# Third layer of a four-layer cross-attention stack: two kinds of stores are issued by ScalarE, and a load is issued later in SyncE's queue

## The chip, the core and the metric

The kernel runs on one core of a Trainium2 chip, in one launch. The metric is the device time of that launch in microseconds (us), as the median of several runs. The engines are TensorE (PE; its weight loads are listed as PEld), VectorE (DVE), ScalarE (ACT), GpSimd (POOL) and SyncE (SP), which in this kernel issues every DMA before the change. Each engine takes its instructions in the order in which they were built and waits at an instruction until the semaphores that it names are reached.

## What is computed

An input x of 8 x 256 tokens with 512 features goes through four cross-attention layers against a context of the same size. In the reference, the third one (the one that changes) reads, with the mask added to the scores:

```python
q = hidden_state @ Wq + bq            # 32 heads of 16
k = encoder_hidden_state @ Wk + bk    # 8 key heads of 16, each for 4 query heads
v = encoder_hidden_state @ Wv + bv
scores = jnp.einsum('bkgld,bksd->bkgls', q, k) * scale + mask
attn = jax.nn.softmax(scores, axis=-1)
out = jnp.einsum('bkgls,bksd->bkgld', attn, v)
out = out @ Wo + bo
x = out + hidden_state                # then a layer norm with gamma and beta
```

The first layer has 16 heads with a feed-forward part, the second a single head, the fourth 16 heads with a layer norm on the context and a gated sum.

## The kernel before, in words

The program is written with a tile framework: pools hand out buffers by tag, and the framework inserts the semaphores. A DMA reports its landing on one of eight completion semaphores, which are handed out in turn to the DMAs of all queues; a DMA is issued only when the last user of its semaphore has landed. A scheduler that runs a timeline at build time decides the order on each engine where the program does not pin it.

The attention of layers one, three and four runs in `pipeline(units, ...)`. A unit of the third layer (`Gqa`) is one of the 8 batch rows `b` and one of four groups `ft` of eight query heads and two key heads, so there are 32 units. The pipeline moves in steps `t` of four chunks. In step `t` it does part A of unit `t`, part B of unit `t-1` and part C of unit `t-2`, and lays other work (projections, the second layer, the contexts, the fourth layer's inputs) between the chunks as fillers under a budget. In steps 2 to 25 TensorE's order is pinned to the written one (`keep_order`); from step 26 the scheduler chooses.

- `load` (L1252, L1253): two loads bring queries into a `stack` tile and keys into a `ks` tile; two stack tiles take turns.
- `A(h)` (L1262, L1272, L1285): products of queries and keys into two "sm" banks, a masked maximum by VectorE, and the negated maxima as a high and a low part in `mhl`.
- `B` (L1293 to L1296): TensorE transposes `mhl`, ScalarE copies it to `mT`, and a DMA writes it as four extra rows, 96 to 99, into the stack tile, so that the next product already has the maxima subtracted.
- `C(i)` (L1315 to L1330): products into two "st" banks, the mask added either by VectorE (L1328) or, after a copy by ScalarE (L1325), by GpSimd (L1326), then ScalarE's exponential (L1330) into a tile `P` or `pk`.
- `D` (L1351 to L1362): the value product `AV` (L636) into the one "av" bank; ScalarE copies it to `xt` (L1355), a DMA stores it to DRAM as `avd` (L1356), and two DMAs load it back as `nd` (L1360), sums and divisors side by side in another layout. These loads wait until the store has landed.
- `E`, some 18 us of planned time later: ScalarE takes the reciprocal of the divisors by two table functions (L1368, L1369), GpSimd multiplies and splits (L1370 to L1373).

Other DMAs of the stage that SyncE issues in the same queue: the stores of keys `k2d` (L1129, six for a batch row) and of queries `q2d` (L422, six) out of two staging tiles `nat`, the loads of the transposed context (L1096) into the same staging tiles, weights (L200), masks (L1578, L1579), and the layer's output (L1528). Before it fills a staging tile (L417 for queries), ScalarE waits until the stores out of it have landed.

Of the kernel before, what the change touches and what calls it, by code (L numbers as in the profile page):

```python
# [8 lines left out]
F = mybir.dt.float32  # L9
# [9 lines left out]
P = 128  # L19
# [9 lines left out]
EL2 = 18.0  # L29
# [19 lines left out]
def S(s):  # L49

    o = []
    for p in s.split(","):
# [9 lines left out]
             P="b5,b0-2", V="v1,v0", vo="b7", nat="b8,b9", h="b10", hc="c0-3", xt="c4-7", bc="c8")  # L62
# [13 lines left out]
def tile_xattn_stack(  # L76
# [31 lines left out]
    nc = tc.nc  # L108
# [54 lines left out]
    def dram(shape, name):  # L163
        return tc.dram_tile(shape, F, name=nm(name))

    def fp(ap):
        return ap.bitcast(F)
# [68 lines left out]
    def feat_mm(pt, ws, ft, xs, n=D):  # L236
        run(feat_steps(pt, ws, ft, xs, n))
        return 12 * n * MMUS

    def tok_mm(pt, xs, tt, ws, n=D):  # L240
        run(tok_steps(pt, xs, tt, ws, n))
        return 12 * n * MMUS


    def feat_g(pt, ws, ft, xs, n=D):
        yield from halves(feat_steps(pt, ws, ft, xs, n), 6 * n * MMUS)
# [103 lines left out]
    fill = Fillers()  # L350
# [134 lines left out]
    avd = [[dram([P, D], "avd") for _ in range(4)] for _ in range(NB)]  # L485
# [129 lines left out]
    class Ring:  # L615
# [4 lines left out]
        def next(self):  # L620
            self.i += 1
            return self.ts[self.i % len(self.ts)]

    def flat(t):
        return fp(t).rearrange("p h t -> p (h t)")
# [23 lines left out]
    class Mha:  # L649
# [1 line left out]

        NCH = 4
        US = 0.6
        ELAG = 2.0

        def __init__(self, ph, st, b, ft, qd, kd, vbias):
            self.__dict__.update(ph=ph, st=st, b=b, ft=ft, vbias=vbias)
# [39 lines left out]
        def B(self):  # L697
            ph = self.ph
            mp = ph.PS("pp")
            nc.tensor.transpose(mp[0:16, 0:P], fp(self.mhl.rearrange("p j c -> p (j c)")), ident)  # L700
            mT = ph.T([32, P], R, "mT")[0:16]
            nc.scalar.copy(mT, mp[0:16, 0:P])
            nc.sync.dma_start(out=flat(self.qs)[97:99], in_=fp(mT))
# [62 lines left out]

    def pipeline(units, before, after, budget, ordered=lambda t: False):
        n, lag = len(units), 2
        late, held = [], []
        prev = [None]  # L770

        def keep_order(first):
            for x in nc.cur_bb.bb.instructions[first:]:
                if x.engine == mybir.EngineType.PE:
                    if prev[0] is not None:
                        tc.add_manual_dep(
                            x,
                            prev[0].name,
                            mybir.DependencyInfo(mybir.DependencyClass.NoSync, mybir.DependencyReason.DATA),
                            reason="keep_order",  # L780
                        )
                    prev[0] = x

        def finish(e):
            units[e].D()
            late.append((fill.now + units[e].ELAG, e))

        for t in range(n + lag + 1):
            fill.step = t
            first = len(nc.cur_bb.bb.instructions)  # L790
            if t == 0:
                before(0)
                units[0].load()
            if t + 1 < n:
                before(t + 1)
                units[t + 1].load()
            u = units[t] if t < n else None
            w = units[t - 1] if 0 <= t - 1 < n else None
            v = units[t - lag] if 0 <= t - lag < n else None
            nch = max(z.NCH for z in (u, v) if z) if (u or v) else 4  # L800
            for i in range(nch):
                us = 0.0
                for z, f in ((u, "A"), (v, "C")):
                    if z and i % (nch // z.NCH) == 0:
                        with tc.high_priority(PRIO):
                            getattr(z, f)(i // (nch // z.NCH))
                        us += z.US
                if i == nch // 2 - 1 and w and not ordered(t):
                    w.B()
                fill.tick(us, budget(t) / nch)  # L810
                if i == 0 and w and ordered(t):
                    w.B()
                while held:
                    finish(held.pop())
                while late and late[0][0] <= fill.now:
                    _, e = late.pop(0)
                    units[e].E()
                    after(e)
            if v:
                if ordered(t):  # L820
                    held.append(t - lag)
                else:
                    finish(t - lag)
            if ordered(t):
                keep_order(first)
            else:
                prev[0] = None
        for _, e in late:
            units[e].E()
            after(e)  # L830
# [219 lines left out]
    cb = bcrow(ph2, "cproj_b")  # L1050
    fill.add(a0_fill())
    pipeline(units0, a0_before, a0_after, lambda t: B0 if 2 <= t < len(units0) else B0E)
    fill.drain()
    ff.ph = ph3
# [13 lines left out]
    for x_ in range(2):  # L1068
        nc.sync.dma_start(
            out=w2od.rearrange("(c r x) n -> x c r n", r=16, x=2)[x_],  # L1070
            in_=w2o.rearrange("(c x r) n -> x c r n", x=2, r=16)[x_],
# [167 lines left out]
    class Gqa:  # L1239
# [1 line left out]

        NCH = 4
        US = 0.8
        ELAG = EL2

        def __init__(self, st, kst, b, ft):
            self.__dict__.update(ph=ph5, st=st, kst=kst, b=b, ft=ft)
# [42 lines left out]
        def B(self):  # L1290
            ph = self.ph
            mp = ph.PS("pp")
            nc.tensor.transpose(mp[0:32, 0:P], fp(self.mhl.rearrange("p u j c -> p (u j c)")), ident)  # L1293
            mT = ph.T([32, P], R, "mT")
            nc.scalar.copy(mT, mp[0:32, 0:P])
            nc.sync.dma_start(out=flat(self.qs)[96:100], in_=fp(mT))  # L1296


        def probs(self):
# [48 lines left out]
        def D(self):  # L1348
            self.av = self.ph.PS("av")
            self.AV()  # L1350
            done2[0] += 1  # L1351
            ph = self.ph
            b, ft = self.b, self.ft
            avs = ph.T([P, D], F, "xt")
            nc.scalar.copy(avs, self.av)  # L1355
            nc.sync.dma_start(out=avd[b][ft], in_=avs)  # L1356
            self.nd = ph.T([P, 2, 256], F, "nd")
            dv = avd[b][ft].rearrange("(g n r) (x t) -> n g r x t", g=4, n=2, x=2)
            for n in range(2):
                nc.sync.dma_start(out=self.nd[:, n, :], in_=dv[n])  # L1360
# [205 lines left out]
    units = [Gqa(ring2, ringk, b, ft) for b in range(NB) for ft in range(4)]  # L1566
# [34 lines left out]
    def after(t):  # L1601
        b = (t % n2) // 4
        if t >= n2 and t % 4 == 1:
            res[b] = take_pair(ph6, h2d[b])
        if t % 4 == 3:
            if t < n2:
                fill.add(l2_post(b, units[t].at), hot=True)
            else:
                fill.until(lambda: "o3" in wts)
                fill.add(proj(ph5, b, units[t].at, wts["o3"], res[b], a3_out), hot=True)  # L1610

    pipeline(
        units,
        lambda t: before2(t) if t < n2 else before3(t),
# [105 lines left out]
```

## Time and profile before

| | |
|---|---|
| runs | 1745.91, 1734.97, 1745.66 us, median 1745.66 |
| profiled execution | 1749.12 us; span of the profile 1747.3 us |
| TensorE busy | 1608.8 us (92% of the span) |
| VectorE, ScalarE, GpSimd busy | 1063.5, 877.1, 772.0 us |
| HBM | 230.79 MB read, 96.49 MB written |

All durations below come from the profiled execution, and the runs' median is 3.5 us under it. In the profile's rows, a line such as L1330 is a line of the kernel printed above; "out<-in" are its tiles with the buffer numbers left out; "idle before" is the time that the engine stood ahead of an instruction, with what released it. SPq is SyncE's queue, which is not counted as busy. PEclk is the granted clock of TensorE, 1.00 being full. A wait for a DMA is named after one DMA on the semaphore that came last, which need not be the one that is meant.

### The profile page before, as it was taken

Reading aid. Unit: us, or ns where it says so; the run is one execution under the profiler, and the core shown is the slowest. Engines: PE = TensorE matmul, PEld = TensorE weight load, DVE = VectorE, ACT = ScalarE, POOL = GpSimd, SP = SyncE. Lnnn points to the kernel's source line nnn. Section 1 sums busy time; section 2 is a strip of 40 time slices with the busy share of each in tenths; the row PEclk is TensorE's granted clock in tenths of the full one; section 3 lists DMA queues with packets and bytes.
Section 4 is the critical chain, followed back from the end, with each engine's and each line's share of the span. In section 5 each row is a group of like instructions: output and inputs, shape, how many; then the busy total and the mean of one; then the engine's idle time right before and its main releaser. Section 6 shows DMA issues by size and latency. Waiting matters only on the chain. (4 is left out here: it accounts for less than half of the span.)

```text
span 1747.3 us, 28325 instructions
## 1 busy us (share of the span) xinstructions
PE 1608.8 (92%) x9984; PEld 1231.5 (70%) x9984; DVE 1063.5 (61%) x2380; ACT 877.1 (50%) x1563; POOL 772.0 (44%) x792
## 2 busy tenths in 40 slices
PE   7999998999899999998889989989878999999998
PEld 6877866777667778887666767667556676778765
DVE  5258556777757766632547767767776774644353
ACT  5335545554545565642346655555564555444454
POOL 6345144323465565532225546555564564312111
PEclk9999998999989999999899999999988899999999
DMA  8879675555542534257657467466264656766562
GB/s 295 310 237 295 208 238 186 165 163 163 171 128 77 176 109 150 80 211 239 219 182 235 162 209 237 159 222 199 93 214 137 202 171 208 231 198 212 183 198 66
DMA packets 168444, 329.16 MB, mean 188 GB/s; under 512 B 16336, under 2 KB 84336, under 8 KB 162800
## 3 DMA queue, kind: packets, MB, share of 16 engines
q1 hardware_dynamic: 168304, 327.35, 58.5%
q8 instruction: 80, 1.31, 0.3%
q14 instruction: 60, 0.49, 0.1%
HBM read 230.79 MB, written 96.49 MB: 187 GB/s over the span
## 5 line engine op out<-in xcount | busy, mean ns | idle before, releaser
L688 DVE TENSOR_REDUCE negm<-sm 128x2 f32<-128x512 f32 x256 | 168.9, 682 | 114.2 <-PE sm L681 113.5
L725 ACT ACTIVATE P<-st 128x512 f32<-128x512 f32 x256 | 144.7, 594 | 111.5 <-PE st L717 108.0
L212 PE MATMUL pp<-ys,fw 128*128 128x512 f32 x768 | 192.6, 401 | 7.4 <-ACT fw L178 3.8
L226 PE MATMUL pp<-pw,gs 128*128 128x512 f32 x768 | 192.0, 397 | 2.9 <-ACT gs L1027 2.6
L636 PE MATMUL av<-P,V 128*32 128x256 f32 (+1 forms) x2204 | 173.7, 408 | 6.0 <-ACT P L1330 3.2
L212 PEld LDWEIGHTS pp<-ys,fw 128*128 128x128 f32 x768 | 145.0, 192 | 42.0 <-ACT fw L178 4.0
L212 PE MATMUL pp<-x,wq 128*128 128x256 f32 x1152 | 160.3, 288 | 9.8 <-ACT wq L181 6.3
L226 PEld LDWEIGHTS pp<-pw,gs 128*128 128x128 f32 x768 | 141.1, 188 | 38.2 <-ACT gs L1027 3.8
L212 PEld LDWEIGHTS pp<-x,wq 128*128 128x128 f32 x1152 | 148.9, 192 | 20.4 <-ACT wq L181 7.3
L1272 DVE CUSTOM_DVE_ANT_0 sm<-sm,va 128x256 f32<-128x256 f32 x256 | 104.0, 443 | 61.6 <-PE sm L1262 61.1
L1272 DVE CUSTOM_DVE_ANT_0 sm<-sm,vb 128x256 f32<-128x256 f32 x256 | 103.9, 443 | 49.2 <-PE sm L1262 48.9
L1028 POOL TENSOR_TENSOR gs<-xt,gs 128x512 fp32r<-128x512 f32 x64 | 91.9, 1444 | 85.7 <-ACT gs L1027 85.7
L1262 PE MATMUL sm<-ks,stack 96*128 96x512 f32 x256 | 101.5, 462 | 17.6 <-DVE mx L1272 7.2
L636 PEld LDWEIGHTS av<-P,V 128*32 128x32 f32 x2204 | 62.5, 110 | 61.8 <-issue 19.5
L226 PE MATMUL pp<-wo,at 128*128 128x512 f32 x384 | 103.2, 404 | 1.3 <-POOL at L1373 0.9
L1023 DVE SCALAR_TENSOR_TENSOR xt<-xt,xt 128x512 f32<-128x512 f32 x64 | 67.5, 1059 | 60.5 <-ACT xt L1022 60.5
L1315 PE MATMUL st<-stack,ks 100*128 100x512 f32 x256 | 88.2, 419 | 14.0 <-DMA stack<-mT 7.7
L693 POOL CAST mhl<-negm 128x8 fp32r<-128x8 f32 x64 | 16.2, 254 | 189.6 <-DVE negm L688 189.6
L1330 ACT ACTIVATE P<-P 128x1024 f32<-128x1024 f32 x77 | 81.4, 1058 | 33.0 <-POOL P L1326 32.9
L179 POOL TENSOR_TENSOR fw<-stg,fw 128x1024 fp32r<-128x1024 f32 x32 | 81.7, 2560 | 35.9 <-ACT fw L178 20.9
L1262 PEld LDWEIGHTS sm<-ks,stack 96*128 96x128 f32 x256 | 47.5, 201 | 63.2 <-issue 50.7
L226 PEld LDWEIGHTS pp<-wo,at 128*128 128x128 f32 x384 | 70.2, 191 | 20.4 <-POOL at L1373 3.1
(215 smaller groups left out, 3622.1 us busy)
## 6 DMA issues: line engine op xcount, KB each, us to landing
stg<-in_wfc_dram SPq DMA_DIRECT2D x32, 512.0 KB
stg<-in_wpr_dram SPq DMA_DIRECT2D x32, 512.0 KB
ws<-med SPq DMA_DIRECT2D x16, 1024.0 KB
ws<-mnd SPq DMA_DIRECT2D x16, 1024.0 KB
q2d<-nat SPq DMA_DIRECT2D x48, 256.0 KB
stack<-q2d SPq DMA_DIRECT2D x32, 384.0 KB
k0d<-nat SPq DMA_DIRECT2D x16, 512.0 KB
stack<-k0d SPq DMA_DIRECT2D x32, 256.0 KB
```

The costliest lines, as they stand in the source:

```text
L179: lo.tensor_tensor(w[:, 1], stg, fp(w[:, 0]), ALU.subtract)
L212: nc.tensor.matmul(pt[:, :n], lhsT=sel(ws, wj, kc)[:, ft * P : (ft + 1) * P], rhs=sel(xs, xj, kc), start=(k == 0), stop=(k == 11),)
L226: nc.tensor.matmul(pt[:, :n], lhsT=sel(xs, xj, kc)[:, tt * P : (tt + 1) * P], rhs=sel(ws, wj, kc), start=(k == 0), stop=(k == 11),)
L636: self.prev = nc.tensor.matmul(o, lhsT=lhsT, rhs=rhs, start=start, stop=stop, skip_group_check=True).ins
L688: nc.vector.tensor_reduce(self.negm[:, 2 * h : 2 * h + 2], pt.rearrange("p (q k) -> p q k", q=2), AX.X, ALU.max, negate=True)
L725: nc.scalar.activation(p, pt, AF.Exp)
L1023: nc.vector.scalar_tensor_tensor(v, v, 1.0 / GA, u, ALU.add, ALU.mult)
L1028: nc.gpsimd.tensor_tensor(lo, u, fp(hi), ALU.subtract)
L1262: nc.tensor.matmul(pts[qt], lhsT=self.qs[0:96, h, qt * P : (qt + 1) * P], rhs=self.ks[0:96].rearrange("p u k -> p (u k)"), start=True, sto ...
L1272: nc.vector.tensor_tensor_reduce(out=t, in0=t, in1=self.am[:, qt, :], scale=1.0, scalar=-3.0e38, op0=ALU.add, op1=ALU.max, accum_out=self. ...
L1315: nc.tensor.matmul(pt, lhsT=self.ks[0:100, u, kt * P : (kt + 1) * P], rhs=self.qs[0:100, 2 * hp : 2 * hp + 2, :].rearrange("p h t -> p (h ...
L1330: last["act"] = nc.scalar.activation(pf, pf, AF.Exp).ins
```

## The change

- The store of the maxima (in `B`) and the store of the value product (in `D`) are issued by ScalarE instead of SyncE: 32 and 32 DMAs. They go to ScalarE's own DMA queue.
- The two loads of `nd` become a part `N` of the unit. `finish` puts a third-layer unit on a list `back` with a count of 2; each chunk lowers the counts, and when one falls below zero, `bring` emits `N` and pins it behind the last SyncE instruction emitted so far. `E` is not emitted before `N`. Units of the other layers have a count of 0 and no `N`.

The tiles, the shapes, the arithmetic and the number of DMAs stay as they are.

```diff
@@ class Mha
-        ELAG = 2.0
+        ELAG, NLAG = 2.0, 0
@@ pipeline
-        late, held = [], []
+        late, held, back = [], [], []
@@
         def finish(e):
             units[e].D()
             late.append((fill.now + units[e].ELAG, e))
+            if units[e].NLAG:
+                back.append([units[e].NLAG, e])
+
+        def bring(e):
+            sp = next(x for x in reversed(nc.cur_bb.bb.instructions) if x.engine == mybir.EngineType.SP)
+            with tc.issue_after(sp):
+                units[e].N()
@@
                 while held:
                     finish(held.pop())
-                while late and late[0][0] <= fill.now:
+                for x in back:
+                    x[0] -= 1
+                while back and back[0][0] < 0:
+                    bring(back.pop(0)[1])
+                while late and late[0][0] <= fill.now and not any(e == late[0][1] for _, e in back):
                     _, e = late.pop(0)
                     units[e].E()
                     after(e)
@@
+        for _, e in back:
+            bring(e)
         for _, e in late:
             units[e].E()
             after(e)
@@ class Gqa
-        ELAG = EL2
+        ELAG, NLAG = EL2, 2
@@ B
             nc.scalar.copy(mT, mp[0:32, 0:P])
-            nc.sync.dma_start(out=flat(self.qs)[96:100], in_=fp(mT))
+            nc.scalar.dma_start(out=flat(self.qs)[96:100], in_=fp(mT))
@@ D
             nc.scalar.copy(avs, self.av)
-            nc.sync.dma_start(out=avd[b][ft], in_=avs)
-            self.nd = ph.T([P, 2, 256], F, "nd")
+            nc.scalar.dma_start(out=avd[b][ft], in_=avs)
+
+
+        def N(self):
+            b, ft = self.b, self.ft
+            self.nd = self.ph.T([P, 2, 256], F, "nd")
             dv = avd[b][ft].rearrange("(g n r) (x t) -> n g r x t", g=4, n=2, x=2)
             for n in range(2):
                 nc.sync.dma_start(out=self.nd[:, n, :], in_=dv[n])
```

## The prediction

> **What bounds the kernel now.** First the page, to see which engine fills the span.
>
> ```profile
> span 1747.3 us, 28325 instructions
> PE 1608.8 (92%) x9984; PEld 1231.5 (70%) x9984; DVE 1063.5 (61%) x2380; ACT 877.1 (50%) x1563; POOL 772.0 (44%) x792
> ...
> PEclk9999998999989999999899999999988899999999
> ```
>
> TensorE is busy for 92% of the span, so a change elsewhere can only move TensorE's idle time and its granted clock. The change touches the third layer alone: its units run from about 840 to 1470 us (first copy of maxima at 848, last sums loaded at 1463). The busy times of that stretch (start:end, length, then busy us of each engine, clock, DMA share, GB/s), and of one short stretch in it:
>
> ```profile
> 840.00:1470.00 630.00, 563.60 (x3168) 411.20 (x3166) 426.07 (x1442) 334.13 (x571) 331.79 (x338) 0.94 0.58 188
> ```
> ```profile
> 1027.40:1034.10 6.70, 5.66 (x22) 2.20 (x23) 1.26 (x7) 2.63 (x3) 1.12 (x1) 0.50 0.73 211
> ```
>
> TensorE idles for 630.0 - 563.6 = 66.4 us here. A mean clock of 0.94 loses another 0.06 x 630 = 37.8 us, in pieces like the second line, where the clock is 0.50 just after TensorE had waited. I price this once: per us of idle time, 37.8 / 66.4 = 0.57 us of clock. So an idle us of TensorE in this stage is worth 1.57 us, more or less.
>
> Then the waits of the same stretch (who <- for whom: total us, times, longest): TensorE's, SyncE's own queue (SPq), ScalarE's.
>
> ```profile
> PE av L636 <- ACT P L1330: 8.5, 7, 2.9
> PE st L1315 <- DMA stack<-mT: 7.7, 3, 4.9
> PE av L636 <- ACT pk L1330: 7.0, 4, 2.1
> ...
> PE st L1315 <- ACT P L1325: 4.2, 3, 3.0
> ...
> PE st L1315 <- ACT pk L1325: 1.5, 2, 1.2
> ```
> ```profile
> SPq L1360 <- DMA avd<-xt: 65.9, 32, 4.7
> SPq L1296 <- ACT mT L1295: 62.2, 20, 16.2
> SPq L1356 <- ACT xt L1355: 55.1, 23, 6.0
> ```
> ```profile
> ACT cx L178 <- DMA nat<-in_ctxT_dram: 11.7, 5, 4.3
> ...
> ACT nat L417 <- DMA ks<-k2d: 10.3, 2, 5.3
> ...
> ACT nat L417 <- DMA k2d<-nat: 7.6, 2, 4.0
> ```
>
> TensorE waits for ScalarE's exponentials and copies in 16 places, 8.5 + 7.0 + 4.2 + 1.5 = 21.2 us, and three times for the maxima, 7.7 us. SyncE stands for 65.9 + 62.2 + 55.1 = 183.2 us of the 630 in front of the three kinds of DMA that the change moves. How that reaches TensorE, in order of time (start, length, engine, line; in brackets the idle time before it and its releaser):
>
> ```profile
> 1002.44 1.17 SPq L1360 DMA_DIRECT2D nd<-avd  x2
> 1003.67 2.42 SPq L1129 DMA_DIRECT2D k2d<-nat  x4
> ```
> ```profile
> 1010.29 0.47 ACT L417 ACTIVATE nat<-pp,bq 128x256 fp32r<-128x256 f32 x1 [5.27 <-DMA ks<-k2d]
> ```
> ```profile
> 1011.76 0.62 PE L636 MATMUL av<-pk,vb 128*32 128x512 f32 x2 [1.90 <-ACT pk L1330]
> ```
>
> Two of six stores of k2d go out at 999.15 and end at 1000.31; SyncE then stands until 1002.44 for the sums to land, issues their two loads, and only from 1003.67 the other four stores. ScalarE waits 5.27 us for the staging tile that they read; the exponential behind that (L1330) comes late, and TensorE loses 1.90 us.
>
> **The change part by part.** What one issue costs, on SyncE (minimum/median/maximum ns):
>
> ```profile
> L1296 SPq DMA_DIRECT2D stack<-mT x32: 666/685/735, 848.3 to 1424.8; - x32
> ```
> ```profile
> L1356 SPq DMA_DIRECT2D avd<-xt x32: 319/338/1067, 892.0 to 1456.9; - x32
> ```
> ```profile
> L1360 SPq DMA_DIRECT2D nd<-avd x64: 500/530/607, 895.5 to 1463.1; - x64
> ```
>
> *(1) ScalarE issues 64 stores.* No ScalarE issue is in the trace; I take SyncE's durations: 32 x 0.685 + 32 x 0.338 = 32.7 us. Each store also waits until the copy before it has left the engine, where now the next copy overlaps it by 0.1 us (the copy of maxima at 1014.55 lasts 0.24, the next one starts at 1014.69): 64 x 0.1 = 6 us. Together 39 us, 0.6 us a store. Behind each stand ScalarE's next copy out of "st" (it frees the bank that TensorE writes next) and the exponentials that the value product waits for. ScalarE has 630 - 334 = 296 us idle here, which is the cover: in the built order a store stands right behind its copy or one or two instructions on, and the next copy has some 2 us until its bank is wanted (the copy of 1015.17 ends at 1015.74; the next product into "st" starts at 1017.87). Where TensorE waits for ScalarE already, 16 places, there is no cover: 16 x 0.6 = 9.7 us, times 1.57 is 15.2. Bounds: 0, if all is covered, and 39 x 1.57 = 61, if nothing is. I take +15.2, since the waits are counted rows.
>
> The Trainium skill ("Perfetto Trace Analysis", DMA Instruction — HWDGE) says that the descriptor generator is shared and locked for one sequencer, and that the issuer is free only when the descriptors are made. That speaks against the change: ScalarE would pay the issue, and sometimes a lock wait as well. The 1067 ns maximum against a median of 338 may be such a case; at 1.07 us for every store part (1) would be 16 x 1.17 x 1.57 = 29 and the whole sum +6.
>
> *(2) SyncE is relieved.* It no longer issues those 64 and no longer stands before them; the 64 loads of sums are issued later, behind whatever SyncE last issued two chunks on. In the built order all six k2d stores then follow each other: the last four start 1003.67 - 1000.31 = 3.4 us earlier, and of the waits on L417 (10.3 + 7.6 = 17.9 us in four batches) 4 x 3.4 = 13.6 go. The transposed context (L1096), queued behind the same q stores, moves up too. If half of TensorE's waits for ScalarE go with that, it is 21.2 / 2 x 1.57 = 16.6. Bounds: 0 (other work of ScalarE and GpSimd ends last) and 21.2 x 1.57 = 33.3. I take -16.6. The loads of sums have cover: issued at 1022.81 now, used by L1368 at 1037.04; if that went, ScalarE would wait (once now: 6.2 us) and the next value product with it.
>
> *(3) The maxima on a queue of their own.* All three waits for them are late in the stage; the largest:
>
> ```profile
> 1306.71 0.67 SPq L1296 DMA_DIRECT2D stack<-mT  x1
> ```
> ```profile
> 1314.95 1.22 PE L1315 MATMUL st<-stack,ks 100*128 100x512 f32 x2 [4.93 <-DMA stack<-mT]
> ```
>
> 8.24 us from issue to use. The store of sums takes about 0.34 + 65.9 / 32 = 2.4 us from issue to landing. If the maxima landed like that from ScalarE, all 7.7 us would go: -7.7 x 1.57 = -12.1. If they landed as late as now, only SyncE's delays before the issue go (0.3 + 1.0 us at the two large ones): -2. I take the middle, -7.0. The Trainium skill ("DMA: Bandwidth & Descriptors", Issuing engines are not separate DMA queues) says that issuing from several engines saves only the issue time, since all run on the same 16 engines; by it this term is near its small end, and the sum -3.4.
>
> *(4) Order.* TensorE's built order is the same for its first 6,060 of 8,610 instructions and from about 7,400 on; between (about 1270 to 1470 us) instructions move by up to 54 places, where the order isn't written by hand. Idle there now: about 28 us. I take 0, with half of it, 14 us, either way.
>
> Sum: 15.2 - 16.6 - 7.0 + 0 = -8.4 us. The profiled execution took 1749.12 us (span 1747.3), so it would be 1740.7; the median of the runs is 1745.66, 3.5 us below, so 1737.3. A measurement here can tell about 1% from no change (17.5 us; the runs of before spread over 10.9).
>
> **The rivals.** *Relief wins:* ScalarE's idle time covers most stores (part 1 at 5), waits behind the staging tiles mostly go (25), and the maxima land early (12.1): -32, 1714 us. For it: 296 idle us on ScalarE, and margins of 9 us and more from the issue of maxima to use in most units. Against: TensorE is 89% busy here, and GpSimd's additions of 1.28 us stand in the same chain.
>
> *No effect:* TensorE and VectorE set the pace, the waits only change their names: 1745 us. For it: five waits of 1.2 us each on "sm" have no releaser and recur once a batch. SyncE may also still stand: eight completion semaphores are shared by both queues, so SyncE can run only eight DMAs past a store that ScalarE hasn't made. Against: by the present times most such places, loads of sums apart, have 6 us of margin.
>
> *Slower:* ScalarE itself stands at its stores. The same sharing makes a store wait until the last user of its semaphore has landed; for 16 stores that is a load of sums, queued on SyncE shortly before. Put at the present times, four of these loads land within 2 us of the copy of maxima that would wait for them (units 9, 13, 17 and 25). If SyncE is late there by its longest such wait, 4.7 us, ScalarE is held 4 x 4.7 = 18.8 us with copies and exponentials behind it, x 1.57 = 29.5, and with -8.4 it is +21: 1767 us. It costs over 1% from a hold of (17.5 + 8.4) / 1.57 / 4 = 4.1 us each; against it, the four depend on the relief of SyncE failing just there.
>
> **How the numbers follow.** Forecast 0.30, no effect 0.14, relief wins 0.32, slower 0.24. The first two lie within 1%, so 0.44; faster by over 1% 0.32; slower 0.24. The range takes the bounds of (1) and (2) in part, up to the two outer cases: 1710 to 1768; within 1% alone it would be 1728 to 1752.
>
> **What would show it.** Right: the waits of L1360 on "avd" and of L1296 on "mT" gone from SyncE; a second queue with 64 issues of 0.34 and 0.69 us on ScalarE; waits of L417 on k2d down from 17.9 to about 5; "st <- stack<-mT" near nothing; TensorE's waits on ScalarE near 20 us. Wrong: ScalarE's issues at over 1 us, waits of several us on ScalarE ahead of them, a stage longer than 630 us, or a clock below 0.94 in it.

## The result and the profile after

The changed kernel takes 1766.17 us, median of four runs (1762.29 to 1768.02), against 1743.74 for the kernel before in the same series (1734.97 to 1745.91). The ratio is 1.0135, 95% interval 1.0094 to 1.0177: some 23 us slower. The forecast was 1737.3. From the page of the changed kernel:

```profile
span 1762.6 us, 28333 instructions
...
PE 1613.0 (92%) x9984; PEld 1235.0 (70%) x9984; DVE 1062.3 (60%) x2380; ACT 877.5 (50%) x1563; POOL 773.5 (44%) x792
...
q10 hardware_dynamic: 5760, 8.92, 1.4%
```

The second queue is there (q10: packets, MB, share), and the busy times of the engines are those of before within 5 us. Of the 15.3 us by which the span grew, TensorE is busy for 4.2, at a lower clock; the rest is idle time. The stage's stretch, and a short one in it (columns as before):

```profile
840.00:1470.00 630.00, 550.78 (x3073) 401.94 (x3071) 417.98 (x1433) 330.26 (x562) 329.74 (x333) 0.92 0.57 180
```
```profile
1025.72:1035.96 10.24, 6.95 (x26) 3.02 (x27) 0.68 (x3) 4.71 (x8) 4.40 (x5) 0.50 0.53 156
```

TensorE is 12.8 us less busy in the same 630 us, at a clock of 0.92 where it was 0.94. The stretch at half clock that lasted about 6.8 us here before now lasts 10.24. TensorE's waits in the stage, then SyncE's largest, then those of ScalarE for transfers (total us, times, longest):

```profile
PE av L636 <- ACT P L1343: 11.1, 4, 5.8
...
PE st L1328 <- ACT P L1338: 8.1, 2, 4.4
PE st L1328 <- ACT pk L1338: 8.1, 6, 3.5
PE st L1328 <- DMA stack<-mT: 7.9, 3, 3.3
...
PE av L636 <- ACT pk L1343: 3.9, 2, 2.4
```
```profile
SPq L1377 <- DMA avd<-xt: 92.1, 13, 15.1
```
```profile
ACT cx L178 <- DMA nat<-in_ctxT_dram: 18.2, 6, 4.7
ACT nd L1385 <- DMA nd<-avd: 12.3, 4, 5.1
...
ACT xt L1368 <- DMA nd<-avd: 5.5, 2, 2.8
...
ACT nat L417 <- DMA k2d<-nat: 4.6, 2, 2.6
```

Four things are to be seen. TensorE's waits for ScalarE's copies and exponentials grew from 21.2 to 31.2 us. The waits for maxima are as they were. SyncE's wait for the landing of the sums' store, which the prediction expected to go, has grown to 92.1 us in 13 waits (65.9 in 32 before); what that costs, no run shows. ScalarE waits less for k2d (17.9 us before, 5.3 with a row of 0.7 for "ks" that isn't shown), but it waits longer for the context (L178; 11.7 before), for late sums (L1385), and in a new row, "xt <- DMA nd". That row is strange at first sight: the copy of sums into "xt" uses nothing of "nd". What waited was the store of maxima ahead of it on ScalarE, which takes its turn on a completion semaphore behind a load of sums: at each of the three stores of maxima that were held, the last DMA issued on the same semaphore was a load of sums, 5.1 to 5.4 us earlier. How such a place looks, at the passage from one batch to the next near 1090 us; SyncE's issues, then ScalarE, then TensorE:

```profile
1080.31 1.83 SPq L1377 DMA_DIRECT2D nd<-avd  x2
...
1082.80 2.29 SPq L422 DMA_DIRECT2D q2d<-nat  x3
1085.18 0.46 SPq L200 DMA_DIRECT2D ws<-med  x1
1085.70 0.85 SPq L1109 DMA_DIRECT2D nat<-in_ctxT_dram  x1
```
```profile
1083.36 0.24 ACT L1308 CAST mT<-pp 32x128 fp32r<-32x128 f32 x1
1085.66 0.64 ACTq L1309 DMA_DIRECT2D stack<-mT  x1
1086.40 0.59 ACT L1368 COPY xt<-av 128x512 f32<-128x512 f32 x1 [2.80 <-DMA nd<-avd]
...
1095.16 1.14 ACT L178 CAST cx<-nat 128x512 fp32r<-128x512 f32 x2 [3.13 <-DMA nat<-in_ctxT_dram]
```
```profile
1098.26 0.80 PE L1328 MATMUL st<-stack,ks 100*128 100x512 f32 x1 [3.53 <-ACT pk L1338]
...
1102.56 1.07 PE L636 MATMUL av<-pk,V 128*32 128x512 f32 x2 [2.43 <-ACT pk L1343]
```

The copy of maxima ends at 1083.60 and its store issues at 1085.66: ScalarE is held for 2.06 us by the load of sums issued at 1080.31, and the copy of sums stands behind it. The context, issued at 1085.70, is used at 1095.16, 9.5 us later (7.8 before), and ScalarE stands 3.13 us for it. Then TensorE loses 3.53 + 2.43 us. There are four such passages, near 957, 1023, 1093 and 1165 us; waits of 0.7 us and more for "st" and "av" cost TensorE 5.8 to 6.8 us in each of them, up to 3.3 before. At the first of the four no store is held; the context is late there, and ScalarE stands 4.7 us for it. From the first product into "st" of unit 0 to the last of unit 31 the layer takes 604.2 us, where it took 587.2.

### The profile page after: what moved, and what is told of

The parts are those of the page before. It is cut to its first block, busy times and chain, and to the rows that moved or that the text cites. A ratio compares the mean times of both kernels' runs of the same rounds, so it can differ in the third digit from the quotient of the medians.

```text
span 1762.6 us, 28333 instructions
## 1 busy us (share of the span) xinstructions
PE 1613.0 (92%) x9984; PEld 1235.0 (70%) x9984; DVE 1062.3 (60%) x2380; ACT 877.5 (50%) x1563; POOL 773.5 (44%) x792
## 4 chain that ended last, share of the span: by engine, by line
PE 31%; DMA 8%; DVE 5%; ACT 3%; issue 2%; SPq 1%; POOL 1%; ACTq 0%; DVEq 0%; POOLq 0%
PE pp L212 7%; PE pp L226 6%; PE av L636 6%; PE sm L1275 3%; PE st L1328 2%; DMA nat<-in_ctxT_dram 2%; PE sm L681 2%; DVE sm L1285 1%; PE st L717 1%; PE pp L1239 1%; PE pp L1194 1%; DMA nd<-avd 1%; DMA stack<-mT 1%; DMA avd<-xt 1%; PE pp L379 1%
## 5 line engine op out<-in xcount | busy, mean ns | idle before, releaser
L212 PE MATMUL pp<-x,wq 128*128 128x256 f32 x1152 | 162.3, 290 | 10.8 <-ACT wq L181 8.1
L1275 PE MATMUL sm<-ks,stack 96*128 96x512 f32 x256 | 101.2, 460 | 16.5 <-DVE mx L1285 7.7
L693 POOL CAST mhl<-negm 128x8 fp32r<-128x8 f32 x64 | 16.2, 254 | 188.3 <-DVE negm L688 188.1
L226 PEld LDWEIGHTS pp<-wo,at 128*128 128x128 f32 x384 | 71.8, 195 | 19.6 <-POOL at L1390 2.5
```

What stands on the lines that cost most here:

```text
L212: nc.tensor.matmul(pt[:, :n], lhsT=sel(ws, wj, kc)[:, ft * P : (ft + 1) * P], rhs=sel(xs, xj, kc), start=(k == 0), stop=(k == 11),)
L226: nc.tensor.matmul(pt[:, :n], lhsT=sel(xs, xj, kc)[:, tt * P : (tt + 1) * P], rhs=sel(ws, wj, kc), start=(k == 0), stop=(k == 11),)
L1275: nc.tensor.matmul(pts[qt], lhsT=self.qs[0:96, h, qt * P : (qt + 1) * P], rhs=self.ks[0:96].rearrange("p u k -> p (u k)"), start=True, sto ...
```

## The experiments

Three numbers are read from each trace. *Part 1* runs from the first product into "st" of unit 0 to that of unit 24, where the order is written out; *part 2* from there to the end of the span, where it is chosen anew for each build. *PE waits* are the rows of TensorE's products into "st" and "av" that wait for ScalarE, 940 to 1180 us (the four passages). From the rows of ScalarE, 840 to 1270 us: waits for the *context*, and *at stores*, where a copy behind a store waits for a transfer that it doesn't use. The upper block has TensorE's order of before throughout (three kernels of it with one or two pairs exchanged); in the lower one the order of part 2 differs. A number in a name counts the units, from the first, that are changed; "tail" means the last 8. The expectations are in microseconds with before near 1744, but the median of before moved between 1739.7 and 1746.2 from series to series; so compare them by the ratio, 0.1% being 1.7 us.

| kernel | ratio [95%] | part 1 | part 2 | PE waits | context | at stores |
|---|---|---|---|---|---|---|
| before | 1 | 436.6 | 453.1 | 12.6 | 11.7 | 0 |
| late_22 | 0.9974 [0.9955, 0.9993] | 429.9 | 447.5 | 11.7 | 15.3 | 0 |
| lag1_22 | 0.9967 [0.9947, 0.9987] | 429.4 | 448.9 | 7.1 | 12.7 | 0 |
| sums_15 | 0.9991 [0.9968, 1.0014] | 438.4 | 447.5 | 16.9 | 21.1 | 2.4 |
| maxima_15 | 1.0003 [0.9978, 1.0027] | 434.5 | 453.1 | 12.4 | 15.1 | 0 |
| busy_17 | 1.0021 [1.0001, 1.0041] | 440.4 | 448.4 | 16.2 | 10.5 | 0 |
| stores_20 | 1.0025 [1.0005, 1.0046] | 439.5 | 448.9 | 16.9 | 12.0 | 0 |
| both_15 | 1.0038 [1.0022, 1.0054] | 439.8 | 447.0 | 21.4 | 17.1 | 5.6 |
| light_15 | 1.0035 [1.0016, 1.0053] | 442.5 | 455.4 | 22.0 | 19.2 | 7.0 |
| both_lag1_20 | 1.0037 [1.0013, 1.0062] | 445.6 | 455.6 | 21.5 | 10.8 | 14.7 |
| | | | | | | |
| after | 1.0135 [1.0094, 1.0177] | 446.3 | 460.0 | 24.7 | 18.2 | 6.6 |
| both_24 | 1.0123 [1.0097, 1.0149] | 449.2 | 463.0 | 24.1 | 19.4 | 6.4 |
| tail_24 | 1.0052 [1.0028, 1.0077] | 433.4 | 461.6 | 14.9 | 13.6 | 0 |
| lag3_15 | 1.0066 [1.0039, 1.0092] | 441.8 | 455.8 | 23.3 | 12.3 | 1.8 |
| spaced_14 | 1.0025 [1.0000, 1.0050] | 440.2 | 457.8 | 17.7 | 14.5 | 3.4 |
| passage_20 | 1.0054 [1.0033, 1.0074] | 441.3 | 453.0 | 16.7 | 22.5 | 0 |
| stores_only | 1.0066 [1.0045, 1.0087] | 448.9 | 454.7 | 21.4 | 11.1 | 2.0 |
| late_loads_only | 1.0039 [1.0020, 1.0058] | 430.9 | 459.5 | 12.1 | 19.2 | 0 |
| ctx_first | 1.0155 [1.0114, 1.0195] | 445.6 | 469.5 | 19.2 | 19.6 | 9.6 |
| before_ctx_first | 1.0013 [0.9988, 1.0038] | 432.4 | 455.6 | 13.3 | 14.5 | 0 |

The parts come from one execution each. Part 1 of before and of tail_24 is the same program and differs by 3.2 us. Part 2 of the ten kernels of the upper block has the same order on all engines, but for single places, and none of the change; it spreads from 447.0 to 455.6 us. So a difference of a few us in these two columns means nothing by itself. The ratios come from many executions. The column "at stores" goes by the rows and isn't exact. Read at the stores themselves, from the end of what ScalarE did before to the issue, the two held stores of maxima in maxima_15 stand 0.9 and 1.1 us, though its column says 0, and no store stands over 0.4 us in stores_only, whose 2.0 us come ahead of a copy.

### First set: each half alone, in all 32 units

*stores_only*: both stores on ScalarE, the load right behind in SyncE's order.

```
-        ELAG, NLAG = EL2, 2
+        ELAG, NLAG = EL2, 0
             nc.scalar.dma_start(out=avd[b][ft], in_=avs)
+            self.N()
```

> ScalarE issues both kinds of stores; the loads of sums stay where they were, right behind the store in the built order. Theory A (the stores on ScalarE cost the time: 64 issues of 0.64 and 0.33 us, and waits for a shared completion semaphore ahead of some): as slow as the changed kernel, 1760 to 1770 us, and at the start of unit 23 at least 5 us behind the kernel before. Theory B (the later loads cost it: they stand in the burst of DMAs ahead of the transposed context, whose landing holds ScalarE and so TensorE): close to the kernel before, 1738 to 1750 us, ScalarE's waits for the context near 12 us.

*late_loads_only*: both stores on SyncE, loads two steps later.

```
-            nc.scalar.dma_start(out=flat(self.qs)[96:100], in_=fp(mT))
+            nc.sync.dma_start(out=flat(self.qs)[96:100], in_=fp(mT))
...
-            nc.scalar.dma_start(out=avd[b][ft], in_=avs)
+            nc.sync.dma_start(out=avd[b][ft], in_=avs)
```

> SyncE issues all stores as before; the loads of sums are issued two chunks later and pinned. Theory A: close to the kernel before or a little faster, 1735 to 1748 us, since SyncE no longer stands before the k2d stores. Theory B: slower, 1755 to 1768 us, ScalarE's waits for the context 16 us or more.

Measured: 1.0066 and 1.0039, between the two theories both times. Neither half makes the loss, and their sum, 1.05%, is near the whole, 1.35%. That was not the answer it seemed: both builds chose their own order for part 2, and late_loads_only is 5.7 us ahead of before in part 1 and loses 6.4 in part 2. What the halves do has to be tried where the order stays.

*ctx_first* and *before_ctx_first*: the context load ahead of the weights "med", in the changed kernel and in the one before.

```
-            self.we = load_hl(ph5, med, "ws")
             self.xs = ph5.T8("cx")
             ...
                 split(stg[:, i], self.xs[i])
+            self.we = load_hl(ph5, med, "ws")
```

> The changed kernel with the load of the transposed context issued ahead of the 1 MB of weights (med) in front of which it stood behind. Theory C (the landing of the context is the gate: what SyncE's relief gains before it is lost in the wait for it, and one long wait of TensorE halves the clock for 10 us): the context lands some 3 us earlier (1 MB at about 350 GB/s), ScalarE's waits for it fall from 18 us to under 8, and the time falls by 12 to 20 us to about 1750 us. Theory A: no such fall, 1760 to 1768 us.

> The kernel before with the same reordering of the context's load. Theory C: its waits for the context (11.7 us) go too, but there is less behind them: 3 to 8 us faster than before, so that the distance to the changed kernel with the same reordering shrinks from 22 to under 12 us. Theory A: the distance stays at 18 to 24 us.

Measured: 1.0155 and 1.0013; theory C fails in both. In the changed kernel ScalarE still stood 19.6 us for the context, since it came to it sooner, and 9.6 us at its stores. Its part 1 is as long as that of after (445.6 and 446.3 us); the 469.5 us of its part 2 belong to yet another order. The context load's place is no cure by itself.

### Second set: the halves and the whole, with TensorE's order kept

The stores' queues and the lag are now set per unit, so that the last units stay as before; with these counts of units the builder gives TensorE the old order.

```
+            k = 4 * b + ft
+            self.NLAG = 2 if k < 15 else 0
+            self.qm = nc.scalar if k < 15 else nc.sync
+            self.qa = nc.scalar if k < 15 else nc.sync
...
+            self.qm.dma_start(out=flat(self.qs)[96:100], in_=fp(mT))
...
+            self.qa.dma_start(out=avd[b][ft], in_=avs)
+            if not self.NLAG:
+                self.N()
```

*both_15* is this; *late_22* has 22 units with late loads and both queues nc.sync; *stores_20* has no late loads and 20 units with both queues nc.scalar.

> Both parts of the change, but only in the first 15 of the layer's 32 units; the other 17 units keep SyncE's stores and loads at once. TensorE's instructions stand as in the kernel before, but for one pair exchanged, so that nothing here comes from another order of the layer's end. Theory H (the parts disturb each other: ScalarE is held at a store of maxima until a late load of sums has landed, and the stores meet the bursts): the stretch of after that these units cover lost about 2 us between units 5 and 14 after a gain of 5 us up to unit 5, so 1741 to 1748 us, holds of about 2 us at units 9 and 13. Theory S (ScalarE's own time for the 64 issues sets the end): 15 units of 1.0 us of issue at up to 1.57 us each, less the relief of SyncE, so 1748 to 1760 us. Theory T (the layer's end, in its other order, holds the loss): 1738 to 1744 us, the same as before or faster.

> Stores on SyncE as before; the loads of sums two steps later in the first 22 units alone. TensorE's, VectorE's and GpSimd's instructions stand in the same order as before. Theories H and T: SyncE's waits ahead of the stores of keys go and nothing is added, the run of all units gained 7.5 us up to unit 22 and lost it after, so 1736 to 1740 us, faster by 0.2 to 0.4 percent. Theory that the loads are late for their user everywhere: 1745 to 1752 us.

> The 40 stores of the first 20 units on ScalarE, each load of sums right behind in SyncE's order; TensorE's order as before. Theory S: 20 units of 1.0 us of issue, at up to 1.57 us: 1750 to 1765 us. Theory H: no hold, since the loads aren't late; SyncE still waits for the sums, so no relief either: 1742 to 1748 us. Theory T: as before, 1741 to 1746 us.

*busy_17* is the kernel before with ScalarE made busy for about as long as the two issues (four copies of 0.30 us, each overlapping the next a little), and nothing else:

```
             nc.sync.dma_start(out=flat(self.qs)[96:100], in_=fp(mT))
+            for _ in range(3 if 4 * self.b + self.ft < 17 else 0):
+                nc.scalar.copy(junk, fp(mT))
             ...
             nc.sync.dma_start(out=avd[b][ft], in_=avs)
+            if 4 * b + ft < 17:
+                nc.scalar.copy(junk, avs[0:32, 0:P])
```

> The kernel before, with four small copies added on ScalarE in each of the first 17 units: three of 0.25 us behind the copy of the maxima and one behind the copy of the sums, about as long as the two issues together (1.0 us), with no store, queue or load moved; TensorE's order is the same but for two pairs. Theory S: 17 us of ScalarE's time at 0.5 to 1.57 us each: 1752 to 1770 us. Theory H or T: ScalarE's time is mostly covered: 1742 to 1748 us.

Measured: late loads alone are faster, 0.26% or 4.5 us. Stores alone cost 0.25%, 4.4 us for 20 units, 0.22 us a unit; a microsecond of plain copies a unit costs 0.21%, 3.7 us for 17 units, also 0.22 us a unit. So the stores by themselves cost about what the same time of ScalarE costs, and some four fifths of that time are covered. The intervals are wide, though (0.04 to 0.40 and 0.01 to 0.42 us a unit), and stores_20 is net of what SyncE gains. By these two, 15 units of both would be 15 x 0.22 - 15 x 0.20 = about 0. Measured is +0.38%, 6.6 us. The halves disturb each other, and they do it in the passages: both_15 has 21.4 us of TensorE's waits there, each half alone 11.7 and 16.9, and before 12.6. Stores of maxima are held 1.7 and 2.1 us at units 9 and 13, as theory H has it.

### Third set: which of the two stores, and which meeting

*sums_15* (only the store of sums on ScalarE) and *maxima_15* (only the store of maxima), both with loads two steps later:

```
-            self.qm = nc.scalar if k < 15 else nc.sync
+            self.qm = nc.sync          # maxima_15: qa instead
```

> First 15 units: sums stored by ScalarE and loaded two steps later, maxima still stored by SyncE; TensorE's order as before. In SyncE's order the store of maxima then stands right behind the context load, ahead of the next loads of weights and sums. Theory Q (it was SyncE's waits at the two stores that kept the next loads away from the context load, and both are gone only with both stores moved): context loads of 7 to 8.5 us from issue to ScalarE's first use, no wait of TensorE over 3 us at the passages, 1734 to 1740 us (relief of SyncE about -3, ScalarE's 15 issues of 0.33 us about +1). Theory H (holds of ScalarE at the store of maxima): that store isn't on ScalarE, so 1734 to 1740 us too. Theory that the late loads and ScalarE's stores of sums meet, whatever SyncE's order: 1743 to 1747 us, as with both stores moved.

> First 15 units: maxima stored by ScalarE, sums stored by SyncE and loaded two steps later; TensorE's order as before. The store of sums stands right behind the context load in SyncE's order and waits there for ScalarE's copy. Theory Q: spacing kept, 1735 to 1742 us (relief -3, 15 issues of 0.64 us about +2). Theory H: ScalarE's store of maxima still takes its turn behind the late loads of sums, holds of about 2 us stay, 1743 to 1747 us.

Measured: 0.9991 and 1.0003; either store alone does no harm that shows, though stores are held in both (0.9 and 0.8 us for the sums, 0.9 and 1.1 us for the maxima). With late loads it takes both stores to lose time that shows.

*lag3_15*: both, the loads three steps later, so that no store of maxima takes its turn behind a load of sums.

```
-            self.NLAG = 2 if k < 15 else 0
+            self.NLAG = 3 if k < 15 else 0
```

> Both stores on ScalarE in the first 15 units, loads of sums three steps later instead of two: by the program's order no store of maxima on ScalarE follows a load of sums on the same completion semaphore, so those holds go; the next loads still stand right behind the context load. Theory H: the loss goes, 1736 to 1742 us. Theory Q: it stays, context loads of 9 to 10 us, TensorE waits of 3 us and more at the passages, 1743 to 1748 us. TensorE's order differs from before only behind the 24th unit.

Measured: 1.0066. That is not to be set against both_15, since part 2 has another order here; part 1 is 441.8 us, 2.0 more than in both_15 and within the spread. No store is held behind a load of sums any more; one of maxima stands 1.0 us behind a store of queries. The first of the two rows below is what took the holds' place (ScalarE, 840 to 1270 us):

```profile
ACT nd L1391 <- DMA nd<-avd: 12.9, 7, 3.2
ACT cx L178 <- DMA nat<-in_ctxT_dram: 12.3, 5, 4.2
```

A load three steps late is late for its user. TensorE still waits 23.3 us in the passages. So the run shows that the holds needn't be there for the passages to be long; it doesn't show that holds cost nothing.

*spaced_14*: both, and SyncE in addition copies the maxima tile to a scratch tensor where it used to store it, behind the context load, so that it stands there again.

```
             self.qm.dma_start(out=flat(self.qs)[96:100], in_=fp(mT))
+            if 4 * self.b + self.ft < 14:
+                nc.sync.dma_start(out=mxd[4 * self.b + self.ft], in_=fp(mT))
```

> Both stores on ScalarE and loads two steps later in the first 14 units, and in each of these units SyncE in addition copies the maxima tile (16 KB) to a scratch tensor that nobody reads, at the place where it stored them before: it waits there again, behind the context load. Everything of the change stays, one transfer more. Theory Q: the passages heal: context loads of 7 to 8.5 us, TensorE's waits of 3.4 and 5.9 us at 957 and 1023 us back to about 2.3, 1738 to 1743 us. Theory H: holds stay, 1743 to 1748 us or more. TensorE's order differs from before in one place early and behind the 24th unit.

Measured: 1.0025, as theory H has it, with an interval that ends just above theory Q; but part 2 has another order (457.8 us). The passages near 1023 and 1093 got shorter (4.1 and 3.3 us of waits; 5.9 and 6.5 in both_15), the one at 957 didn't (6.1). Undecided by time.

### Fourth set: where in the layer, and on what

*both_24* and *tail_24*: the whole change in the first 24 units, or in the last 8.

```
both_24: self.NLAG = 2 if k < 24 else 0    # qm, qa alike
tail_24: self.NLAG = 0 if k < 24 else 2    # qm, qa alike
```

> The whole change in the first 24 units, the last 8 as before. Theory Q (the loss is made in the passages from batch to batch, at units 5, 9, 13 and 17, about 4 us each beyond the parts): 1752 to 1760 us. Theory T (most of the loss is made in the layer's end): 1743 to 1750 us.

> The change in the last 8 units alone, the first 24 as before. Theory Q: 1742 to 1752 us, at most a third of the loss. Theory T: 1753 to 1762 us. TensorE's order differs from before behind the 24th unit, as it does in the changed kernel, but not in the same way.

Measured: 1.0123, above both theories, and 1.0052, between them; together they are more than the whole. The reason is in part 2. It is 463.0 us in both_24, whose last 8 units carry nothing of the change, 461.6 in tail_24 and 460.0 in after; with the old order it was 447.0 to 455.6, mean of ten 450.5. So these builds lose some 10 us at the layer's end whether the stores there are moved or not. What differs there in both_24 is the order that the builder chose. Most of it is lost while the last 8 units run: from unit 24 to the last product into "st" of unit 31 it is 157.9 us in after, 155.1 in both_24, 153.9 in tail_24, and 144.7 to 150.6 with the old order.

*light_15*: both_15 without the mask loads (two of 256 KB) of batches 2 and 3, so that the passages near 957 and 1023 carry less.

```
+        if b not in (2, 3):
             nc.sync.dma_start(out=am, in_=amask[b]...)
             nc.sync.dma_start(out=amT, in_=amaskT[b]...)
```

> Both parts in the first 15 units, and the two mask loads (256 KB each) of batches 2 and 3 left out, so that the softmax of these batches works on the masks of the batches before: the passages at about 957 and 1023 us carry 0.5 MB less, the one at about 1093 us is unchanged; TensorE's order as with both parts and the masks. Theory Q: TensorE's waits at the first two passages (5.9 and 3.4 us with the masks) come down to about 2, the third stays at about 4 us; time 1738 to 1743 us. Theory H (ScalarE held, whatever the transfers): all three stay, 1744 to 1748 us.

Measured: 1.0035, and neither lightened passage got shorter. TensorE's row for "av", 940 to 1180 us, in light_15 and then in both_15:

```profile
PE av L636 <- ACT P L1347: 10.9, 3, 6.4
```
```profile
PE av L636 <- ACT P L1347: 10.1, 3, 5.9
```

The longest is still the wait at the first passage. The masks' bytes are not what makes the passages long: this expectation failed.

*lag1_22*: stores on SyncE, loads one step later instead of two, in 22 units.

> Stores on SyncE, the loads of sums one step later instead of two, in the first 22 units; TensorE's order as before. If the relief needs only that the sums' store has landed when SyncE comes to the loads (2 to 3 us): 1736 to 1741 us, as with two steps. If a load still waits a step later: 1741 to 1746 us.

Measured: 0.9967, as the first expectation has it, and with 7.1 us of waits in the passages the lowest ratio of the study; the interval of late_22 overlaps it. The same passage as above, SyncE, ScalarE, TensorE:

```profile
1071.47 1.17 SPq L1383 DMA_DIRECT2D nd<-avd  x2
...
1080.83 0.37 SPq L1109 DMA_DIRECT2D nat<-in_ctxT_dram  x1
1081.26 0.68 SPq L1313 DMA_DIRECT2D stack<-mT  x1
```
```profile
1078.59 0.24 ACT L1312 CAST mT<-pp 32x128 fp32r<-32x128 f32 x1
1079.89 0.59 ACT L1372 COPY xt<-av 128x512 f32<-128x512 f32 x1 [1.06 <-PE av L636]
...
1088.28 1.14 ACT L178 CAST cx<-nat 128x512 fp32r<-128x512 f32 x2 [2.68 <-DMA nat<-in_ctxT_dram]
```
```profile
1091.39 0.80 PE L1332 MATMUL st<-stack,ks 100*128 100x512 f32 x1 [0.51 <-ACT pk L1342]
...
1094.82 1.06 PE L636 MATMUL av<-pk,V 128*32 128x512 f32 x2 [1.57 <-ACT pk L1347]
```

The loads of sums are out 9.4 us before the context instead of 5.4, with stores of keys and queries and other loads between; the context is used 7.5 us after its issue; 1.30 us lie between the starts of the copy of maxima and of the next copy, where after has 3.04; and TensorE waits 0.51 + 1.57 us instead of 3.53 + 2.43.

### Fifth set: both, without one or the other meeting

*passage_20*: both in 20 units, but in each batch row the store of maxima and the store of sums that stood right behind the context load stay on SyncE.

```
-            self.qm = nc.scalar if k < 20 else nc.sync
-            self.qa = nc.scalar if k < 20 else nc.sync
+            self.qm = nc.scalar if k < 20 and ft != 1 else nc.sync
+            self.qa = nc.scalar if k < 20 and ft != 3 else nc.sync
```

> The change in the first 20 units, but in each batch row the one store of maxima and the one store of sums that SyncE issued right behind the context load stay on SyncE, in their old place; the other 30 stores go to ScalarE, loads two steps later. Theory Q (SyncE's waits at these two kept the next loads off the context load): TensorE's two waits of 3 to 4 and 2.4 us in a passage fall to about 1 to 1.5 and 2, the context load's time to first use to 7 to 8.5 us, and the time to 1740 to 1748 us (30 stores at 0.1 us, relief of SyncE -3 to -4). Rival (the loads two steps late and ScalarE's stores anywhere): 1752 to 1760 us. TensorE's order differs from before only behind the 24th unit.

Measured: 1.0054. No row of a hold at stores is left, and TensorE's waits for ScalarE are 16.7 us, but ScalarE stands 22.5 us for the context, the most of all. The theory that these two stores on SyncE keep the context load fast fails: it took 8.0 to 8.9 us from issue to use, where it took 6.8 to 7.8 before. The time is that of the rival, with another order in part 2 (453.0 us).

*both_lag1_20*: all 40 stores on ScalarE, loads one step later.

```
-            self.NLAG = 2 if k < 20 else 0
+            self.NLAG = 1 if k < 20 else 0
```

> All 40 stores of the first 20 units on ScalarE, loads of sums one step later instead of two; TensorE's order as before. Theory Q: nothing of SyncE's waits is left behind the context load, so the passages stay long, waits of 3 to 4 and 2.4 us, 1750 to 1757 us. Rival (it is the two steps: loads that meet the passage's burst): 1741 to 1747 us, waits as with the stores on SyncE.

Measured: 1.0037, at the low end of theory Q, with an interval that reaches the rival. Here the context is as fast as before (6.3 to 7.6 us), and ScalarE stands at its stores instead. The passage once more, and ScalarE's rows:

```profile
1082.58 0.24 ACT L1312 CAST mT<-pp 32x128 fp32r<-32x128 f32 x1
1086.23 0.64 ACTq L1313 DMA_DIRECT2D stack<-mT  x1
1086.96 0.59 ACT L1372 COPY xt<-av 128x512 f32<-128x512 f32 x1 [4.14 <-DMA q2d<-nat]
```
```profile
ACT xt L1372 <- DMA q2d<-nat: 11.8, 3, 4.2
ACT cx L178 <- DMA nat<-in_ctxT_dram: 10.8, 6, 3.4
```

The turn on the shared semaphores has moved by one load, and now it is a store of queries, in the same burst, for which the store of maxima waits: it stands 3.4 us, and ScalarE is idle for 4.14 us ahead of the copy of sums.

## Why the prediction was wrong, by its own steps

**The price of a wait was too high.** Against before, TensorE's waits for ScalarE in the passages grew by 24.7 - 12.6 = 12.1 us; at 1.57 that would be 19 us, but part 1 grew by 9.7 (11.3 if tail_24's reading is averaged in), 0.8 to 0.9 us for each us of wait. The upper block says the same: from lag1_22 (7.1 us, 0.9967) over stores_20 (16.9, 1.0025) to both_15 (21.4, 1.0038) the ratio rises with this column, with sums_15 (16.9, 0.9991) as the exception, and a straight line through the ten has 0.83 us for each us. With 0.83 in place of 1.57 the prediction's own counts, 9.7 and 10.6 us of waits, would have given +8.1 for (1) and -8.8 for (2). That is an estimate, but it is near what both measured.

**(1) ScalarE issues 64 stores: mis-sized by itself, too high.** The issues last 636 and 326 ns:

```profile
L1309 ACTq DMA_DIRECT2D stack<-mT x32: 636/637/1236, 846.6 to 1440.5; - x32
```
```profile
L1369 ACTq DMA_DIRECT2D avd<-xt x32: 320/326/352, 889.3 to 1471.9; - x32
```

What they cost is 0.22 us a unit, at that rate 7 us in 32, where +15.2 was taken. The warning drawn from the Trainium skill ("Perfetto Trace Analysis", DMA Instruction — HWDGE), that the issuer may wait for a lock as well, would have put this term at 29 us. The trace shows no such wait on ScalarE: only one of the 64 issues is long, 1.24 us, and it is the first store of maxima. So it is, with 1.21 to 1.25 us, in all thirteen kernels in which ScalarE stores the maxima, wherever that first store stands; why the first is long stays open.

**(2) SyncE relieved: right in kind, too high.** The waits on L417 went from 17.9 to 5.3 us, as expected. Not as described, however: SyncE's wait for the sums' landing is 59.9 us in late_22 and 58.9 in lag1_22, little under the 65.9 of before; most of it has not gone, though no longer between the stores of k2d. Alone the relief is worth 4.5 to 5.8 us in 22 units (late_22, lag1_22), at that rate 6.5 to 8.4 in 32, where -16.6 was taken. "The loads of sums have cover" failed with the rest of the change in place: ScalarE waits 12.3 us for them now, 6.2 before.

**(3) Maxima on their own queue: failed.** TensorE's waits for them are 7.9 us (7.7 before), where 7.0 of gain were taken. At the passage near 1013 us, unit 9, the store took 7.96 us from issue to landing; before it was 6.58. The trace agrees here with the Trainium skill ("DMA: Bandwidth & Descriptors", Issuing engines are not separate DMA queues), by which this term would have been near its small end, -2.

**(4) Order: mis-sized.** Taken at 0 with 14 us either way; part 2 is 460.0 us, 9.5 over the mean of those with the old order. This is two fifths of the loss. That it is the order is argued and not shown; neither a kernel with the change in 24 units and the old order in part 2 was run, nor one with after's order and no change. The nearest are lag3_15, spaced_14 and passage_20, which have in part 2 one and the same order of TensorE and of ScalarE, another than before's, and nothing of the change: 455.8, 457.8 and 453.0 us, on average 5 us over the old order. So an order alone can cost about half of it.

**The step that failed is the sum.** It added (1) and (2) as if they were independent. Measured alone they nearly cancel; together they lose 6.6 us in 15 units. In the first 24 units, by what each measured, (1) would cost 24 x 0.22 = 5.3 us, (2) would gain 4.9 or a little more and (3) nothing, about 0 in all; part 1 grew by 9.7 to 11.3 us. That is what the halves do to each other: 6.6 us in 15 units make 10.6 in 24 (an estimate by units). The other 9.5 us lie in part 2, where the order and the same disturbance in the last 8 units are not told apart; with them it is some 20 of the 23 us. ScalarE works in program order through the passages, and there it now has two more places to stand for transfers of the same burst: its stores take their turn on completion semaphores shared with SyncE's loads (2.06 us at 1085.66), and the late loads of sums stand in SyncE's order ahead of the context, which comes later (9.5 us from issue to use, 7.8 before). When one is taken away, the rows show ScalarE standing at the other: lag3_15 (for late sums), both_lag1_20 (for stores of queries), passage_20 (for the context). No kernel with both stores on ScalarE gained. How much of the 10 us each place makes is not shown.

**The rival "slower"** gave 1767 us, and 1766 came; its mechanism is only part of it. It named the holds at units 9, 13, 17 and 25 at 4.7 us each. They are there at 9, 13 and 17, with 1.7, 2.1 and 1.9 us, not at 25. At 1.57 these 5.7 us are 9 of the 23, at 0.83 they are 5. The number was right by luck: a smaller hold, slower contexts and another order at the end, the last two not in it, add up to the same.

**What stays open:** why the context load takes 8 to 10 us from issue to use where it took 6.8 to 7.8. It isn't a matter of both halves: late_22, with all stores on SyncE, has 7.0, 8.2, 8.2 and 9.7 us in the four passages, and with loads one step later it is 6.2 to 7.6 whoever issues the stores (lag1_22, both_lag1_20). The third passage of late_22, SyncE and ScalarE:

```profile
1075.14 0.78 SPq L1109 DMA_DIRECT2D nat<-in_ctxT_dram  x1
```
```profile
1083.35 1.14 ACT L178 CAST cx<-nat 128x512 fp32r<-128x512 f32 x2 [2.89 <-DMA nat<-in_ctxT_dram]
```

So the slow load goes with the two steps, though stores_20, without late loads, has 9.1 us twice as well. Nor does it cost time by itself, since late_22 is faster than before: there the context is also issued sooner. Counted from the first product into "st" of units 4, 8, 12 and 16, ScalarE uses it after 15.6, 15.7, 14.5 and 15.5 us in before, 16.5, 14.0, 13.9 and 14.5 in late_22, but 19.5, 16.7, 16.5 and 17.8 in after. The cause is not the masks' bytes (light_15), and not only the two stores behind it (passage_20).

## What to carry over

A store moved to a computing engine cost little here while it was only its issue, 0.22 us of 1.0; look instead for what it may be made to wait on there, since everything behind it on that engine waits too. Two edits that touch the same burst of transfers must be costed together: here one was worth -0.3%, the other +0.25%, and both, in fewer units, +0.4%. The way to see it was to keep the other engines' order fixed and to change only as many units as that allowed; the first, whole-layer halves were blurred by an order chosen anew: part 2 of the kernels with another order is 2 to 19 us over the mean of those with the old one.

## What the runs showed of the hardware that was not expected

ScalarE's issue is as long as SyncE's (637 and 326 ns against 685 and 338). A store of 16 KB landed after 7.96 us in a burst, from a queue of its own. The first store of maxima that ScalarE issues takes 1.21 to 1.25 us in every kernel, the others 0.64. Where TensorE waits longer in a passage, the stretch at half clock is mostly longer: 10.24 us in all four passages of after, 13.65 in two of both_24, at most 6.8 in those of before. It isn't one long wait alone that decides it: lag1_22 has a stretch of 10.24 us near 1093 us, where its waits for ScalarE are 0.51 and 1.57 us. The stretches come in pieces of 3.4 us (3.41, 6.83, 10.24, 13.65), each of which, at half clock, costs at most 1.7 us of full-speed work.
